# Macaron block on one core: feed-forward features and power sums written by column tiles, statistics a turn earlier

## The chip, the cores and the metric

The program runs on one core of a Trainium2 chip. Its engines work side by side, each through its own instructions in order: TensorE (PE in the profile; its weight loads are PEld), VectorE (DVE), ScalarE (ACT), GpSimd (POOL) and SyncE (SP), which here issues nearly all transfers between memory and the chip. TensorE writes only to PSUM; the others move its results on. The metric is the device time of one launch in microseconds. Three runs of the kernel before took 3954.24 us in the median (3950.4 to 3954.5).

## The reference

Four sequences of 512 tokens with 512 features pass a half-weighted feed-forward network, an attention layer of the gated delta kind, and the same feed-forward network again:

```python
x = x + 0.5 * ffn(layernorm(x), gate_cp, up_cp, down_cp)
x = x + attn(layernorm(x), W_qkvz, W_ba, conv_w, dt_bias, A_log, norm_w, W_out)
x = x + 0.5 * ffn(layernorm(x), gate_cp, up_cp, down_cp)

def ffn(h, gate_cp, up_cp, down_cp):        # layernorm: (x - mean) / sqrt(var + 1e-5)
    gate_w = spline(gate_cp)                # 2048 x 512
    up_w = spline(up_cp)                    # 2048 x 512
    down_w = spline(down_cp)                # 512 x 2048
    return (silu(h @ gate_w.T) * (h @ up_w.T)) @ down_w.T
```

Each weight matrix is a cubic spline through some 8,100 control points, about 129 weights to a segment. So 128 neighbouring weights of a row lie on one or two cubic pieces. The kernel uses that: a product with such weights needs only few combinations of the inputs. The attention is not touched by the change and takes the middle of the run.

## The kernel before

`ffn(src, dst, build)` runs twice, with `attention()` between. The first time it also builds the spline weights (`build`), the second time it loads them. In both, `B` is 4 sequences. `NC` and `NT` are 4 (chunks of 128 features, tiles of 128 tokens), `NB` is 16 (blocks of 128 hidden rows), `NG_F` is 8, `NODES` and `BLK` are 32, `P` is 128 and `S` is 512. One sequence goes through these steps:

- **Features** (`features`, lines 344 to 380). `norm(t)` normalises a tile of 128 tokens on VectorE (L355); its first call computes the statistics of the whole sequence (`statistics`, L331 to L342: BN statistics on VectorE, L336 and L337, then the power -1/2 on GpSimd, L341). `turn(t)` transposes the tile on TensorE (L362) and ScalarE copies it (L363). `interpolate(hf, c)` multiplies a 128 x 128 slice of the table `lag` with chunk `c` (L367). Its 128 output rows are 32 for each of four feature groups, but a later matmul wants, for one group, the 32 rows of all four chunks in one tile `ft[g]`. So ScalarE copies the result to a staging tile `fs` (L371, four buffers), and four transfers put its quarters into four `ft` tiles (L373). That is 8 matmuls, 8 copies and 32 transfers.
- **Hidden** (`hidden`). For each of 16 blocks a gate and an up matmul (L435, 128 x 128 x 512), SiLU on ScalarE (L442), their product on VectorE (L444), and a store of the block to `hid` in memory (L445). `gu` PSUM has two buffers, `ffn_it` has four.
- **Gather** (`gather`). Sixteen indirect transfers on GpSimd (L454) read the rows of `hid` back in another order into the tiles `nat`. The first waits until all of `hid` is stored.
- **Project** (`project`). 32 units: four `sums(k)`, each four matmuls of 32 columns (L474) with the table `pw` (powers of the position), one per `nat` tile, into the four quarters of a PSUM tile; ScalarE copies it (L478) to `fs`, and four transfers (L481) put 16 rows of each quarter into a tile `fm`. Then 16 `blocks(v)` (L491, four matmuls of 32 rows each), four `rest(g)` (L494) and eight `total(k, g)` (L497), which add up in four PSUM banks `y`. `back(g)` transposes the result (L508) and VectorE adds it to the residual `ffn_xr` in 44 steps (L536). The output is then stored (L514).

**Order.** A small calendar delays followers: `later(d, f)` runs `f` after `d` further `tick()`s. The first sequence's features and hidden blocks, and the second's features (`whole`), are issued ahead of the loop, in an order that a planner finds. From there `manual_schedule` keeps the written order on TensorE, VectorE, ScalarE and GpSimd; SyncE's order is still the planner's. In turn `b` of the loop the 16 gathers of sequence `b` come first on GpSimd. Then the 32 gate and up matmuls of hidden(b+1) are issued one by one, as slots. Woven between: `norm` for sequence b+2 at slots 0 to 3; from slot 2, up to slot 12 (`lead`), the back-transposes of sequence b-1 with the turns and interpolations of b+2; from slot 12 the units of project(b). Sequence b+2 is loaded at the start of the same turn. In turn 2 there is no sequence 4 to prepare, and the loop then issues hidden(3) first and the units of project(2) behind it, with the last 16 gathers dropped in between; turn 3 is project(3) alone.

The loop that sets this order, at the end of `ffn`, begins:

```python
nat, steps = gather(0)
for b in range(B):
    for f in steps:
        f()
    main, norms, turns, inter = [], [], [], []
    if b + 1 < B:
        main = hidden(b + 1, ft)
    if b + 2 < B:
        ft, norms, turns, inter = features(load(b + 2, "ffn_x", io))
    units, back = project(b, nat)
```

## Time and profile before

| | us |
|---|---|
| median of 3 runs | 3954.24 |
| the profiled execution | 3989.9 |
| its span, first to last instruction | 3988.1 |
| TensorE matmul busy (90% of the span) | 3608.3 |
| VectorE, ScalarE, GpSimd busy | 2628.2, 1472.2, 857.1 |
| first feed-forward stage, from to | 0 to 460 |
| second feed-forward stage, from to | 3587 to 3988 |

An engine row gives busy time in tenths of each of 40 equal slices (99.7 us each); `PEclk` is the clock that TensorE was granted, in tenths. A row of stretches has the stretch, its length, then busy time and instruction count of PE, PEld, DVE, ACT and POOL, the granted clock, the share of the transfer engines and GB/s. A timeline row has start, duration, engine, line, operation, output<-inputs and count; in brackets stands how long the engine was idle before it and what released it. A chain row has start, duration, engine, name and line. One matmul in the code is two instructions in the profile ("x2"), and four small ones are "x8". SPq and POOLq mark the issuing of transfers.

### The profile page before, as it was taken

The page shows a single profiled execution, that of the slowest core. Times are in us where ns is not written, and L with a number is a line of the kernel's source. Part 1 is how long each engine was busy: PE and PEld are TensorE (multiplying, and loading weights), DVE is VectorE, ACT ScalarE, POOL GpSimd, SP SyncE. Part 2 cuts the span into 40 slices and gives each one's busy share as a digit, 9 for nine tenths or more (in the row PEclk, how much of TensorE's full clock was granted, in tenths as well). Part 3 has the DMA queues.
Part 4 walks back from the last instruction along what each step waited for, and adds up shares of the span by engine and source line. Part 5 has one row for each costly group of instructions (what it writes and reads, how often), then busy time and mean ns, then how long its engine had stood idle before and what let it go on. Part 6 is the DMA issues. An engine that isn't in the chain of part 4 may idle for free. (4 is left out here: it accounts for less than half of the span.)

```text
span 3988.1 us, 62538 instructions
## 1 busy us (share of the span) xinstructions
PE 3608.3 (90%) x24184; PEld 2005.3 (50%) x24184; DVE 2628.2 (66%) x5925; ACT 1472.2 (37%) x3448; POOL 857.1 (21%) x662
## 2 busy tenths in 40 slices
PE   5878668999999999999999999999999999976788
PEld 2333325555555555555555555555555555542333
DVE  5222267887787888777878887787888877632221
ACT  2321113444444444444444444444444444422221
POOL 2113011222222222222222222222222222111111
PEclk7989778999999999999999999999999999978898
DMA  5535211221112222221222221122121121115353
GB/s 175 179 120 181 91 44 51 64 67 58 57 57 73 59 83 59 65 59 57 62 70 80 62 67 58 56 62 70 57 85 56 53 67 54 48 72 189 112 170 94
DMA packets 319192, 323.25 MB, mean 81 GB/s; under 512 B 102736, under 2 KB 237168, under 8 KB 318320
## 3 DMA queue, kind: packets, MB, share of 16 engines
q1 hardware_dynamic: 308656, 285.69, 23.3%
q0 software_dynamic: 10240, 33.56, 2.9%
q8 instruction: 191, 3.13, 0.3%
q14 instruction: 105, 0.86, 0.1%
HBM read 247.60 MB, written 50.59 MB: 75 GB/s over the span
## 5 line engine op out<-in xcount | busy, mean ns | idle before, releaser
L981 DVE SCALAR_TENSOR_TENSOR acc<-pj,cw,acc 128x511 f32<-128x511 f32 (+2 forms) x768 | 573.6, 747 | 151.6 <-ACT acc L979 133.4
L971 PE MATMUL pj<-xnT,w_v 128*128 128x512 f32 x1024 | 521.1, 602 | 0.0
L1286 PE MATMUL pz<-w_z,xnT 128*128 128x512 f32 x1024 | 514.6, 614 | 0.0
L1434 PE MATMUL py<-w_o,gT 128*128 128x512 f32 x1024 | 513.7, 615 | 0.4
L444 DVE TENSOR_TENSOR ffn_it<-pu,ffn_sg 128x512 f32<-128x512 f32 x128 | 88.5, 691 | 332.1 <-PE pu L435 194.5
L971 PE MATMUL pj<-xnT,w_k 128*128 128x512 f32 x512 | 265.3, 626 | 20.2 <-DMA w_k<-in_L_attn_W_qkvz 20.2
L971 PE MATMUL pj<-xnT,w_q 128*128 128x512 f32 x512 | 255.3, 602 | 0.0
L989 ACT ACTIVATE th<-acc 128x512 f32<-128x512 f32 x256 | 163.0, 637 | 235.4 <-DVE acc L981 226.3
L1342 ACT ACTIVATE tq<-pks,rqe 128x128 f32<-128x128 f32 x384 | 120.3, 364 | 339.9 <-DVE rq L1183 204.9
L1412 ACT ACTIVATE oo<-oo,orr 128x128 f32<-128x128 f32 x512 | 162.6, 389 | 206.5 <-POOL oo L1407 206.5
L979 ACT ACTIVATE acc<-pj,cw 128x512 f32<-128x512 f32 x256 | 175.3, 685 | 170.2 <-PE pj L971 169.4
L454 POOL DMA_INDIRECT nat<-hid,idx x128 | 122.0, 953 | 490.4 <-PE y_pt L508 160.6
L1434 PEld LDWEIGHTS py<-w_o,gT 128*128 128x128 f32 x1024 | 171.0, 191 | 106.2 <-issue 95.2
L1286 PEld LDWEIGHTS pz<-w_z,xnT 128*128 128x128 f32 x1024 | 169.8, 191 | 99.5 <-issue 88.5
L1012 POOL TENSOR_TENSOR rsq<-msq,phalf 128x4 f32<-128x4 f32 x64 | 64.8, 1013 | 684.8 <-DVE msq L1010 684.8
L1012 POOL TENSOR_TENSOR rsk<-msk,phalf 128x4 f32<-128x4 f32 x64 | 70.0, 1094 | 653.3 <-DVE msk L1010 651.7
L971 PEld LDWEIGHTS pj<-xnT,w_v 128*128 128x128 f32 x1024 | 170.7, 191 | 70.7 <-issue 64.1
L1168 POOL TENSOR_TENSOR ks<-kn,ws 128x1024 f32<-128x1024 f32 x64 | 122.5, 1915 | 379.2 <-DVE ws L1161 346.7
L993 DVE SCALAR_TENSOR_TENSOR vT<-th,acc 128x512 f32<-128x512 f32 x128 | 181.7, 1420 | 23.1 <-ACT th L989 23.1
L1093 DVE TENSOR_TENSOR inv<-inv,inv_tmp 128x30 f32<-128x30 f32 (+14 forms) x480 | 168.8, 352 | 16.5
L1400 DVE TENSOR_REDUCE om<-osq 128x4 f32<-128x512 f32 x128 | 87.1, 681 | 138.5 <-ACT osq L1399 138.5
L1350 PEld LDWEIGHTS pzz<-rr,tt 128*128 128x128 f32 x768 | 114.9, 193 | 113.3 <-issue 54.5
(204 smaller groups left out, 6923.6 us busy)
## 6 DMA issues: line engine op xcount, KB each, us to landing
hid<-ffn_it SPq DMA_DIRECT2D x128, 256.0 KB
w_v<-in_L_attn_W_qkvz SPq DMA_DIRECT2D x64, 512.0 KB
w_z<-in_L_attn_W_qkvz SPq DMA_DIRECT2D x64, 512.0 KB
w_o<-in_L_attn_W_out SPq DMA_DIRECT2D x32, 1024.0 KB
ab<-decay_c SPq DMA_DIRECT2D x64, 512.0 KB
ft<-fs SPq DMA_DIRECT2D x256, 64.0 KB
w_k<-in_L_attn_W_qkvz SPq DMA_DIRECT2D x64, 256.0 KB
w_q<-in_L_attn_W_qkvz SPq DMA_DIRECT2D x64, 256.0 KB
```

The source lines that it names most:

```text
L454: nc.gpsimd.indirect_dma_start(out=nt, out_offset=None, in_=to[:, :], in_offset=bass.IndirectOffsetOnAxis(ap=idx[:, v : v + 1], axis=0),)
L971: nc.tensor.matmul(pj, w()[:, c, col : col + DK], xnT[:, c, :], start=c == 0, stop=c == NC - 1)
L979: nc.scalar.activation(acc, pj, AF.Copy, scale=cw[:, ch, 3:4])
L981: nc.vector.scalar_tensor_tensor(acc[:, d:], pj[:, : S - d], cw[:, ch, 3 - d : 4 - d], acc[:, d:], ALU.mult, ALU.add)
L989: nc.scalar.activation(th, box["acc"], AF.Tanh)
L993: nc.vector.scalar_tensor_tensor(dest(), box["th"], 1.0, box["acc"], ALU.add, ALU.mult)
L1012: nc.gpsimd.tensor_tensor(rs, ms, phalf[:, :NT], ALU.pow)
L1093: nc.vector.tensor_tensor(ee[:, j + 1 :, :j], ee[:, j + 1 :, :j], tj, ALU.add)
L1168: nc.gpsimd.tensor_tensor(ks, bc(kn, 2, 2), bc(ws, 3, P), ALU.mult)
L1286: nc.tensor.matmul(pz, xnT[:, c, t * P : (t + 1) * P], pair["wz"][:, c].rearrange("p j k -> p (j k)"), start=c == 0, stop=c == NC - 1,)
L1412: nc.scalar.activation(s["oo"][:, t, r], s["oo"][:, t, r], AF.Copy, scale=s["orr"][:, u : u + 1])
L1434: nc.tensor.matmul(box["py"], pair["gT"][r][:, t, :], pair["wo"][:, r, :], start=r == 0, stop=r == 3)
```

## The change

- `interpolate` is now per feature group `g`: four matmuls of 32 columns each, one per chunk, write the four quarters of one PSUM tile, which ScalarE copies straight to `ft[g]`. The 32 transfers and `fs` go.
- `sums`: two calls share a PSUM tile. `pw` becomes two tables of 32 columns; the second has the powers in columns 16 to 31 and zeros elsewhere. Call r = 0 starts each quarter and r = 1 adds to it, and one copy writes the whole tile `fm`. The 16 transfers go. The gathered tiles that one call reads are 8m + 2j + r for j = 0 to 3, where before they were four neighbours.
- `statistics` is its own step `stats`. In the loop, sequence b+3 is loaded at slot 16 of turn `b` and its statistics are issued at slot 28, so they stand ahead of the next gathers on GpSimd.
- The loop body becomes `turn_of(b)`. The 16 gathers of the next sequence are issued at the end of a turn. In turn 2 the units of project(2) are woven into hidden(3) too, except the last 16, which follow the gathers.
- In the building stage, the second sequence's features are woven into hidden(0) from its ninth slot. In the other stage hidden(0) is a turn -1 in the hand-written order, with the same features.
- SyncE belongs to the hand-written order as well.

```diff
@@ -347,9 +347,10 @@
                 ft = [fp.tile([P, S], F32, name="ft") for _ in range(NG_F)]
                 xn, stat = {}, {}
 
+                def stats():
+                    stat["mv"], stat["rstd"] = statistics(xt)
+
                 def norm(t):
-                    if t == 0:
-                        stat["mv"], stat["rstd"] = statistics(xt)
                     mv, rstd = stat["mv"], stat["rstd"]
                     xn[t] = wk.tile([P, H], F32, name="ln_xn", bufs=3)
                     nc.vector.tensor_scalar(
@@ -362,26 +363,22 @@
                         nc.tensor.transpose(pt[:, c, :], xn[t][:, c * P : (c + 1) * P], ident)
                     later(1, lambda: nc.scalar.copy(xnT[:, :, t * P : (t + 1) * P], pt))
 
-                def interpolate(hf, c):
+                def interpolate(g):
                     pf = ps.tile([P, S], F32, name="pf", tag="tp")
-                    nc.tensor.matmul(pf, lag[:, c, hf * P : (hf + 1) * P], xnT[:, c, :], start=True, stop=True)
-
-                    def spread():
-                        fs = wk.tile([P, S], F32, name="fs", tag="fs", bufs=4)
-                        nc.scalar.copy(fs, pf)
-                        for q in range(4):
-                            nc.sync.dma_start(
-                                ft[4 * hf + q][NODES * c : NODES * (c + 1)], fs[NODES * q : NODES * (q + 1)]
-                            )
-
-                    later(1, spread)
+                    for c in range(NC):
+                        nc.tensor.matmul(
+                            pf[NODES * c : NODES * (c + 1)], lag[:, c, NODES * g : NODES * (g + 1)], xnT[:, c, :],
+                            start=True, stop=True,
+                        )
+                    later(1, lambda: nc.scalar.copy(ft[g], pf))
 
                 turns = [lambda t=t: turn(t) for t in range(NT)]
-                inter = [lambda hf=hf, c=c: interpolate(hf, c) for hf in range(2) for c in range(NC)]
-                return ft, [lambda t=t: norm(t) for t in range(NT)], turns, inter
+                inter = [lambda g=g: interpolate(g) for g in range(NG_F)]
+                return ft, stats, [lambda t=t: norm(t) for t in range(NT)], turns, inter
 
             def whole(xt):
-                ft, norms, turns, inter = features(xt)
+                ft, stats, norms, turns, inter = features(xt)
+                stats()
                 for n_, t_ in zip(norms, turns):
                     n_()
                     t_()
@@ -410,9 +407,11 @@
             wr = wdp.tile([P, NB, P], F32, name="wr")
             we = wdp.tile([P, H], F32, name="we")
             cm = wdp.tile([P, 2, H], F32, name="cm")
-            pw = wdp.tile([P, BLK], F32, name="pw")
+            pw = wdp.tile([P, 2, BLK], F32, name="pw")
             idx = wdp.tile([P, NB], mybir.dt.int32, name="idx")
-            nc.sync.dma_start(pw, grid[:, G_POW:G_IDX])
+            nc.vector.memset(pw, 0.0)
+            for e in range(2):
+                nc.sync.dma_start(pw[:, e, 16 * e : 16 * e + 16], grid[:, G_POW : G_POW + 16])
             nc.sync.dma_start(idx, grid[:, G_IDX:].bitcast(mybir.dt.int32))
             if not build:
                 nc.sync.dma_start(wr.rearrange("p c h -> p (c h)"), wr_d)
@@ -469,18 +468,15 @@
                     if k == 0:
                         box["xr"] = load(b, "ffn_xr", ip)
                         box["fm"] = [np_.tile([P, S], F32, name="fm", tag="fm", bufs=2) for _ in range(2)]
-                    pf = ps.tile([P, S], F32, name="pm", tag="tp")
+                    m, r = divmod(k, 2)
+                    if r == 0:
+                        box["pm"] = ps.tile([P, S], F32, name="pm", tag="tp")
+                    pm = box["pm"]
                     for j in range(4):
-                        nc.tensor.matmul(pf[BLK * j : BLK * (j + 1)], pw, nat[4 * k + j], start=True, stop=True)
-
-                    def spread():
-                        fs = wk.tile([P, S], F32, name="fs", tag="fs", bufs=4)
-                        nc.scalar.copy(fs, pf)
-                        for j in range(4):
-                            at = 16 * (4 * (k % 2) + j)
-                            nc.sync.dma_start(box["fm"][k // 2][at : at + 16], fs[BLK * j : BLK * j + 16])
-
-                    later(1, spread)
+                        at = slice(BLK * j, BLK * (j + 1))
+                        nc.tensor.matmul(pm[at], pw[:, r], nat[8 * m + 2 * j + r], start=r == 0, stop=r == 1)
+                    if r:
+                        later(1, lambda: nc.scalar.copy(box["fm"][m], pm))
 
                 def blocks(v):
 
@@ -543,61 +539,92 @@
                 units += [lambda k=k, g=g: total(k, g) for k in range(2) for g in range(4)]
                 return units, [lambda g=g: back(g) for g in range(4)]
 
-            for f in hidden(0, ft):
-                f()
-                tick()
-            drain()
-            built.close()
+            plan = {"nxt": None, "tail": [], "ft": ft}
+
+            def turn_of(b):
+
+
+                main = hidden(b + 1, plan["ft"]) if b + 1 < B else []
+                norms, turns, inter = [], [], []
+                if plan["nxt"]:
+                    plan["ft"], _, norms, turns, inter = plan["nxt"]
+                    plan["nxt"] = None
+                units, back = [], []
+                if b >= 0:
+                    units, back = project(b, plan["nat"])
+                plan["nat"], steps = gather(b + 1)
+                tail, early = plan["tail"], []
+                for i in range(4):
+                    early += [*tail[i : i + 1], *turns[i : i + 1]]
+                early += inter
+                lead = 6 * 2 if b >= 0 else len(main)
+                for i, f in enumerate(main):
+                    if b + 3 < B:
+                        if i == 16:
+                            xt = load(b + 3, "ffn_x", io)
+                        if i == 28:
+                            plan["nxt"] = features(xt)
+                            plan["nxt"][1]()
+                    for n_ in norms[i : i + 1]:
+                        n_()
+                    f()
+                    tick()
+                    n = -(-len(early) // max(1, lead - i)) if i < lead else 0
+                    if i >= 2 or not turns:
+                        for f in early[:n]:
+                            f()
+                            tick()
+                        early = early[n:]
+                    if i >= lead:
+                        keep = 16 if b + 2 == B else 0
+                        n = -(-(len(units) - keep) // (len(main) - i))
+                        for f in units[:n]:
+                            f()
+                            tick()
+                        units = units[n:]
+                drain()
+
+                for f in steps if b + 1 < B else ():
+                    f()
+                for f in early + units:
+                    f()
+                    tick()
+                plan["tail"] = back
+
+            by_hand = lambda: tc.manual_schedule(
+                engines={e.engine for e in (nc.tensor, nc.vector, nc.scalar, nc.gpsimd, nc.sync)}
+            )
+            if B > 1:
+                xt = load(1, "ffn_x", io)
+                plan["nxt"] = features(xt)
+                plan["nxt"][1]()
+            if build:
+                first = hidden(0, plan["ft"])
+                ft, _, norms, turns, inter = plan["nxt"] or (None, None, [], [], [])
+                more = [f for nt in zip(norms, turns) for f in nt] + inter
+                xt2 = load(2, "ffn_x", io) if B > 2 else None
+                for i, f in enumerate(first):
+                    f()
+                    tick()
+                    for f in more[:1] if i >= 8 else ():
+                        f()
+                        tick()
+                        more = more[1:]
+                drain()
+                plan["ft"], plan["nxt"] = ft, None
+                if B > 2:
+                    plan["nxt"] = features(xt2)
+                    plan["nxt"][1]()
+                built.close()
             np_ = st.enter_context(tc.tile_pool(name="ffn_nat", bufs=NB + 4))
-            ft = whole(load(1, "ffn_x", io)) if B > 1 else None
-            tail = []
-            with tc.manual_schedule(engines={e.engine for e in (nc.tensor, nc.vector, nc.scalar, nc.gpsimd)}):
...
+            with by_hand():
+                if build:
+                    plan["nat"], steps = gather(0)
                     for f in steps:
                         f()
...
+                for b in range(0 if build else -1, B):
+                    turn_of(b)
+                for f in plan["tail"]:
                     f()
                     tick()
                 drain()
```

## The prediction

> **What bounds the kernel.** I began with the rows of tenths: attention (about 460 to 3587 us of the span) keeps TensorE near nine tenths and is not touched; the two feed-forward stages have holes. Then one row per stage of the second one, cut where a turn's first gate matmul starts. "Turn 0" is hidden(1) with project(0) woven in, "turn 1" hidden(2) with project(1).
>
> ```profile
> PE   5878668999999999999999999999999999976788
> PEclk7989778999999999999999999999999999978898
> ```
>
> ```profile
> core 0: us, PE busy (x) PEld busy (x) DVE busy (x) ACT busy (x) POOL busy (x), PEclk, DMA share, GB/s
> ...
> 3661.25:3755.08 93.83, 71.76 (x280) 28.23 (x279) 12.60 (x20) 20.29 (x36) 16.41 (x17) 0.87 0.45 138
> 3755.08:3856.33 101.25, 75.29 (x295) 30.32 (x294) 22.57 (x74) 20.39 (x36) 16.25 (x17) 0.87 0.43 130
> 3856.33:3977.23 120.90, 109.55 (x477) 43.59 (x475) 25.26 (x112) 19.52 (x33) 30.31 (x32) 0.90 0.43 141
> ```
>
> TensorE is the busiest engine by far, and a turn holds 22 to 26 us in which it stands. The timeline of turn 1 says why:
>
> ```profile
> 3757.75 0.60 PE L508 MATMUL y_pt<-ident,yg 128*128 128x128 f32 x4
> 3758.26 1.02 POOL L454 DMA_INDIRECT nat<-hid,idx  x1 [75.54 <-DMA hid<-ffn_it]
> ...
> 3777.10 0.95 POOL L454 DMA_INDIRECT nat<-hid,idx  x1 [0.30 <-issue]
> 3778.07 1.04 POOL L341 TENSOR_TENSOR ln_rstd<-ln_var,phalf 128x4 f32<-128x4 f32 x1
> 3779.15 1.00 DVE L355 TENSOR_SCALAR ln_xn<-ffn_x,ln_mv,ln_rstd 128x512 f32<-128x512 f32 x2 [20.37 <-issue]
> 3779.84 1.09 PE L362 MATMUL ln_pt<-ident,ln_xn 128*128 128x128 f32 x4 [21.49 <-DVE ln_xn L355]
> ```
>
> The power for 1/std (1.04 us on GpSimd) sits behind 16 gathers, 1.25 us apart. Normalising on VectorE waits for it, the transposes wait for that, and TensorE, in written order, waits 21.5 us with ready matmuls behind. A second hole comes later in the turn:
>
> ```profile
> 3798.39 7.47 SPq L373 DMA_DIRECT2D ft<-fs  x12
> ...
> 3802.29 0.59 ACT L371 COPY fs<-pf 128x512 f32<-128x512 f32 x1 [2.38 <-DMA ft<-fs]
> ...
> 3803.43 1.12 PE L435 MATMUL pg<-ft,wc 128*128 128x512 f32 x2 [2.33 <-ACT ffn_sg L442]
> ```
>
> Each feature copy is followed by four transfers at 0.6 us of SyncE; the fifth copy needs a staging buffer back, and the SiLU and then the gate matmul queue behind the copy.
>
> **Cost of a column-tiled group.** The chain shows four 128x32 matmuls of 512 columns (two passes each, x8) beside a full one (x2):
>
> ```profile
> 3716.19 1.07 PE y L491 x8
> 3717.26 1.00 PE pm L474 x8
> 3718.26 1.05 PE pg L435 x2
> ```
>
> Here a group takes 1.00, elsewhere 1.12; a full matmul is 0.86, 1.05 right after tiled work. Against the change speaks the Trainium skill, "TensorEngine Tiling (Array Packing)", Key Properties: changing the tiling mode drains the engine, and the new features do so 16 times per sequence. It states no figure. But the row already stands between two switches: at worst 1.12 for the group and 1.05 - 0.86 on the full matmul behind it, 1.31. So a group costs 1.00 to 1.31, most rows lie near the low end, and I take 1.06: 8 x (1.06 - 0.86) = +1.6 us per sequence, 13 in all. Were the rule a further price, say one 0.43 us pass at each switch, it would be 7 us per sequence, 55 in all, and the forecast 3825 would read 3880; nothing in the row asks for that.
>
> **Part 1, statistics one turn sooner.** Moved are 4 x (0.67 + 0.18) + 0.17 = 3.6 us of VectorE, 1.04 us of GpSimd and the 1 MB load of x on SyncE. The load goes from the gathers' time to slot 16 of the turn before, in a stretch at 66 to 74 GB/s; 12 slots of over 1 us cover it. The power now stands ahead of the gathers, whose own start still waits for the last hidden store (3758.26, about 3.2 us after the turn's first matmul). Removed are the waits: 19.6 + 1.8 (restart at half pace) in turn 0, 21.6 + about 2.5 in turn 1. The power moved ahead of 16 gathers delays none of them, since they start later than it ends. Queued behind the moved statistics is ffn_it of that slot, hence the next up matmul: 3.6 us less about 2 of slack, 1.5 us, three times (4.5; bounds 0 to 11).
>
> **Part 2, no chip transfers.** 384 SyncE issues of about 0.6 us and 21 MB go; one clearing of the power table and one more small load per stage come, at a start where larger loads cover them. What returns to TensorE is the copy wait: from 3702.45 to 3715.06 there are 7.7 us of work in 12.6 (4.9 us) in turn 0, and likewise 7.3 us in turn 1. PSUM copies: eight for features stay eight; sums need two for four, 1.2 us of idle ScalarE. The sums still run 16 small matmuls; their accumulation needs gathers 8, 10, 12, 14 for the third sum (before 8 to 11). Gather 14 is issued about 3.2 + 14 x 1.25 + 1 = 21.7 us into a turn and lands by 24 to 26; TensorE reaches that sum at 12 x 0.86 + 1.75 + 1.75 + 8.5 + 0.86 + 2 + 0.86 + 1.07 = 27. Hidden barely; I charge 1 us in each of four turns (0 to 5).
>
> So turn 0 becomes 93.8 - 19.6 - 1.8 - 4.9 + 1.6 = 69.1, turn 1 101.25 - 21.6 - 2.5 - 7.3 + 1.6 = 71.5. Sums of rows agree: hidden 27.5, turns 1.75, features 8.5, sums 4, blocks 15.5 and switches 1.6, rest and totals 10.3, which is 69.2. In the first stage the same turns last 80.6 (gathers started under other work) and 101.1.
>
> **Part 3, the last two turns.** Before, from 3856.33 to 3975.5: 119.1 us, as hidden(3) runs with nothing between (1.97 us a pair against 1.72, and 8 us of waits) and each projection runs alone (37.5 us each). After: hidden(3) 27.5 + back-transposes 1.75 + 16 units 17 + pace 1.4 = 47.6. Then 16 kept units (14.3 us), under which the last gathers start 3.2 us in. TensorE is at the third sum of project(3) after 14.3 + 1.75 + 2 + 1.07 + 3.2 (the y banks wait for VectorE, as before) = 22.3; gather 14 lands near 25.5, after which 27 us of projection remain: 53. Together 100.6, a gain of 18.5; in the first stage 123.3 - 100.6 = 22.7. Without the kept units as cover, the gather wait would be 14 us longer.
>
> **Part 4, starts.** Second stage, first features to turn 0: 52.75. After: eight groups 8.5, hidden 27.5, turns 1.75, features 8.5, VectorE pace 2.2, about 0.6 at the seams: 49, gain 3.7. In the first stage hidden(0) with the weight build is 71.2 us and whole(1) follows to 88.7; woven in, 10.3 us of TensorE work goes partly into gaps of 0.9 us per two blocks: 79 (76 to 84), gain 9.7. At its very start, four late feature matmuls (44.57 to 48.2) held the coefficient transposes 5.5 us; VectorE and GpSimd follow (0 to 6), I take 3. SyncE by hand inside the stages: behind the output store, which waits for the 44 VectorE additions, stand the hidden stores; four buffers of 3 us and more cover it. At the seams with attention the weight loads may no longer pass the last store: -4 to +4 us, taken as 0.
>
> **What comes new.** Hidden stores now share the transfer engines with the gathers. "DMA: Bandwidth & Descriptors", Issuing engines are not separate DMA queues, says that transfers from any issuing engine share 16 engines and interleave, and this speaks against the change. The trace has one such stretch, hidden(3) over gathers:
>
> ```profile
> 3867.79 11.86 SPq L445 DMA_DIRECT2D hid<-ffn_it  x4
> ...
> 3878.61 0.69 DVE L444 TENSOR_TENSOR ffn_it<-pu,ffn_sg 128x512 f32<-128x512 f32 x1 [6.92 <-remote]
> ...
> 3879.36 2.07 PE L435 MATMUL pu<-ft,wc 128*128 128x512 f32 x2 [3.25 <-issue]
> ```
>
> It lost 8.0 us idle and about 2 cold. By the rule as full competition, each of six turns (three a stage) pays 10, and the forecast would be 3870. By pace, the new turns store every 3.7 us against 2 and load no residual meanwhile: I take 2.5 x 6 = 15 (0 to 60).
>
> **Sum**, against the profiled span of 3988.1 (execution 3989.9): 3 + 9.7 + 11.5 + 29.6 + 22.7 + 3.7 + 24.7 + 29.7 + 18.5 = 153.4; less 15 + 4.5 + 4 = 23.5: 129.9. The median shown, 3954.24, is 0.991 of that execution, so 128.7 off it: **3825**.
>
> **Rivals.** (a) *Stores and gathers collide fully*: 60 for 15, late gathers 16 for 4: net 73, 3882. For it, transfers at 0.91 share there; against it, half the store rate and 21 MB fewer bytes. (b) *All is covered*: none of the 23.5 appears, 3802. (c) *Slower*: the feature tiles do not overlap. Four in a row cost 3.44 a group, 2.38 more x 64 = 152, net +22: 3976. It decides from 1.06 + 130/64 = 3.1 us a group. The sums' tiles of the same shape overlap, though each has its own moving tile where the features' four read slices of one. (d) *The change doesn't do what it says*: the 21 us wait only moves from the transposes to the sums, in three turns 63 us: net 67, 3888. For it, the sums wait for the same gathers; against it, they come 23 to 27 us into a turn.
>
> **Chances.** Main case 0.55 (3802 to 3850), (a) 0.20 (3850 to 3900), (b) 0.17 (3780 to 3802), (c) 0.04, (d) 0.04. A measurement of this kernel tells some 0.2% from no change; a quarter of (c), tiles that overlap partly, ends within it: faster 0.96, within 0.01, slower 0.03. The range 3783 to 3876 leaves out about 2 in 10: half of (a), (c), (d) and the low edge of (b).
>
> **What would show it.** Right: ln_rstd before the first gather, ln_pt with no wait on ln_xn, turns of 70 to 75 us in the second stage, feature groups near 1.06 us, no staging rows. Wrong: feature matmuls of 3 us a group, hidden stores late for ffn_it by 8 us a turn, or sums waiting on gathers. The forecast falls most easily on the 15 us for transfers and on the last gathers.

## The result, and the profile after

The changed kernel took **3886.7 us** in the median (3884.7 to 3887.2); the kernel before, beside it, took 3954.3 (3950.4 to 3954.5). The ratio is 0.983, with an interval of 0.9813 to 0.9847. It is faster by 68 us where the forecast said 129, and it ends above the range.

The pictures of the two executions differ by more than that: the spans are 3988.1 and 3885.4, a difference of 102.7. The rest of this document is about these two gaps. One has to know for it that the runs fall into two kinds, by the chip they met: on some the kernel before takes 3948 to 3958 us in the median, on others, called the slower chips below, 3976 to 3987. Each time is therefore compared with the kernel before on the same chip; where stretches of two chips are put side by side, the text says so.

First the tenths of TensorE and of its clock, after the change:

```profile
PE   5998569999999999999999999999999999987998
PEclk7999679999999999999999999999999999997999
```

Attention fills the middle as before; both ends have filled up. The stretches of the second feed-forward stage, cut at the same instructions as before (turn 0, turn 1, turns 2 and 3; the columns are those explained above):

```profile
core 0: us, PE busy (x) PEld busy (x) DVE busy (x) ACT busy (x) POOL busy (x), PEclk, DMA share, GB/s
3613.14:3685.79 72.65, 71.76 (x326) 24.69 (x327) 16.45 (x30) 18.55 (x33) 16.97 (x18) 1.00 0.45 149
3685.79:3757.49 71.70, 71.70 (x343) 26.48 (x342) 19.19 (x65) 19.33 (x34) 15.20 (x16) 1.00 0.42 147
3757.49:3872.60 115.11, 103.53 (x461) 36.58 (x460) 23.95 (x105) 16.60 (x28) 30.26 (x32) 0.97 0.44 149
```

Turn 1 has no idle time left. The timeline of its start shows why; this answers the rows in which the transposes waited 21.5 us:

```profile
3682.57 1.04 POOL L341 TENSOR_TENSOR ln_rstd<-ln_var,phalf 128x4 f32<-128x4 f32 x1 [45.79 <-DVE ln_var L339]
3688.88 1.02 POOL L453 DMA_INDIRECT nat<-hid,idx  x1 [5.27 <-DMA hid<-ffn_it]
...
3688.90 0.60 PE L363 MATMUL ln_pt<-ident,ln_xn 128*128 128x128 f32 x4
...
3695.49 1.06 PE L369 MATMUL pf<-ffn_xnT,lag 128*32 128x512 f32 x8
```

The power is done 5.3 us before the first gather, the transposes carry no wait, and a feature group costs the 1.06 us of the forecast. What is new is in the waits of TensorE (engine and line, what it waited for, us in total, times, longest), first stage and then second:

```profile
PE pm L477 <- DMA nat<-hid,idx: 14.8, 8, 5.8
...
PE pm L477 <- DMA nat<-hid,idx: 11.1, 7, 3.7
```

The power sums wait for gathered tiles, 15 times. The kernel before has no such row in the run before_c (below), whose profile gives the landings of its gathers; the profile of the forecast gives none, so its silence alone would not say much. Stage by stage, in us of the two profiled executions:

| stretch | before | after | forecast |
|---|---|---|---|
| FFN1: hidden(0), features(1) | 88.7 | 76.0 | 79 |
| FFN1: turn 0 | 80.6 | 79.9 | 69.1 |
| FFN1: turn 1 | 101.1 | 71.7 | 71.5 |
| FFN1: turns 2 and 3 | 123.3 | 116.6 | 100.6 |
| FFN2: first features to turn 0 | 52.8 | 52.7 | 49 |
| FFN2: turn 0 | 93.8 | 72.7 | 69.1 |
| FFN2: turn 1 | 101.3 | 71.7 | 71.5 |
| FFN2: turns 2 and 3 | 119.0 | 115.1 | 100.6 |

The holes that the change aimed at are gone at the price forecast. Turns 2 and 3 are 16.0 and 14.5 us too long, turn 0 of the first stage 10.8.

### The profile page after: what moved, and what is told of

Same layout as the page of the kernel before. It is cut to its first block, busy times and chain, and to the rows that moved or that the text cites. A ratio compares the mean times of both kernels' runs of the same rounds, so it can differ in the third digit from the quotient of the medians.

```text
span 3885.4 us, 62488 instructions
## 1 busy us (share of the span) xinstructions
PE 3594.6 (93%) x24568; PEld 1975.0 (51%) x24568; DVE 2631.4 (68%) x5927; ACT 1463.3 (38%) x3432; POOL 855.7 (22%) x662
```

## Experiments

**Parts alone, on one chip (kernel before there: 3987.3).** Theory: the stage table, with the excess put down to sums that wait for gathers. Rivals: transfers that collide (rival a), and a start value that does not hold. First the kernel before once more.

> The kernel before, unchanged. Its first profiled execution took 3989.9 us, its other runs 3950 to 3955. If that one execution was slow by chance, this one shows about 3955, and a comparison by stages says where 35 us went. If it is bound to the profile (for instance because this kernel issues many more transfers), it is again near 3990 while the runs beside it stay near 3954. My forecast assumed a slowdown spread evenly over the whole run.

3987.4 us, span 3985.5: on this chip the first profile is the ordinary case, and the 3954 of the median is not. Stage by stage the two profiles agree as well (turns 2 and 3 take 123.7 and 117.3 us here, 123.3 and 119.0 there). On which chip the first was taken is not on record; that it was one of the slower kind is a conclusion from these times.

The column tiles alone, in the order of before:

```diff
-                    nc.tensor.matmul(pf, lag[:, c, hf * P : (hf + 1) * P], xnT[:, c, :], start=True, stop=True)
...
+                    for c in range(NC):
+                        nc.tensor.matmul(
+                            pf[NODES * c : NODES * (c + 1)], lag[:, c, NODES * g : NODES * (g + 1)], xnT[:, c, :],
```

> The kernel before with column-tiled features and sums and no chip transfers; loop, statistics and SyncE's order as before. By my steps: the staging waits go (about 19 us in four turns and some 15 at the stage starts), the tiles cost 13, the wait of the power behind the gathers stays: 20 us off, 3934. If the sums then wait for gather 14 in place of the staging waits, nothing is left: 3950 to 3955.

3954.8 us, ratio 0.992 (0.9906 to 0.9939): 32.5 us gained, more than the 20 of its first theory; 14.7 of them lie between hidden(0) and turn 0 of the first stage. The statistics alone, one turn sooner, staging and transfers kept:

```diff
+                            if i == 16:
+                                xt = load(b + 3, "ffn_x", io)
+                            if i == 28:
+                                nxt = features(xt)
+                                nxt[1]()
```

> The kernel before with load and statistics one turn sooner and nothing else. By my steps the 21 us wait goes in three turns and 5 us in the fourth: up to 65 us off, 3890. If the wait only moves to the sums, which need the same gathers, a third of it is left: 3930 or more.

3956.2 us, ratio 0.992 (0.9907 to 0.994): 31 us, less than half of the 66.9 us for which the transposes wait in the first profile (4.7, 21.5, 19.3 and 21.5), and between what the two theories gave. A stand, that is a stretch of idle time, like that of the run after_again, below, takes 10.5 and 11.1 us of the two second turns. Then the changed kernel with each pair of sums moved behind eight blocks, so that the sums that read gathers 8 to 15 come last:

```diff
-                units = [lambda: sums(0), lambda: sums(1), lambda: blocks(0), lambda: sums(2)]
-                units += [lambda v=v: blocks(v) for v in range(1, 4)] + [lambda: sums(3)]
+                units = [lambda v=v: blocks(v) for v in range(NB // 2)] + [lambda: sums(0), lambda: sums(1)]
+                units += [lambda v=v: blocks(v) for v in range(NB // 2, NB)] + [lambda: sums(2), lambda: sums(3)]
```

> The changed kernel with the sums moved behind the blocks of the same gathered tiles (two after the eighth block, two after the sixteenth), and the residual's load with them. If late gathers are what the last two turns and the first stage's turn 0 lost (in its profile 8 us in that turn, about 5 in each turn 2 and 8 to 10 in each turn 3), 25 to 35 us go: 3852 to 3862. If the last turns are long by tile switches and VectorE's pace, at most 8 go: 3879 or more.

3929.7 us, ratio 0.986 (0.984 to 0.9873): by its ratio no better than the change itself, and far from the 3852 to 3862 of its first theory. Turn 1 takes 85.3 and 85.2 us in the two stages instead of 71.7, with a stand of 11.1 and 9.6 us in front of the first feature group. This profile gives no landing of a gather, so it cannot tell whether the sums still waited. The changed kernel was then run on such a chip too.

**Suspected transfers, on a chip where the kernel before takes 3982.5.**

> The changed kernel unchanged, beside its variants on one chip. Theory 1 (what a chip adds lies on both kernels alike): ratio to the kernel before again 0.981 to 0.985, so about 3887 us where the kernel before takes 3954, and about 3920 us where it takes 3987. Theory 2 (the changed kernel meets nothing of what makes the kernel before slower there): 3887 us on either, a ratio of 0.975 where the kernel before takes 3987.

3930.5 us, ratio 0.988 (0.9847 to 0.9907), nearer to theory 1; the changed kernel loses on such a chip as well, 44 us against 28. Its stretches, and the place in turn 1 of the first stage that the last one starts from:

```profile
3623.65:3706.56 82.91, 73.22 (x326) 25.01 (x327) 16.45 (x30) 18.43 (x33) 16.96 (x18) 0.94 0.40 130
3706.56:3792.06 85.50, 74.35 (x344) 26.86 (x343) 19.28 (x65) 19.22 (x34) 15.18 (x16) 0.94 0.37 123
3792.06:3911.02 118.96, 106.19 (x461) 38.00 (x460) 24.45 (x105) 16.48 (x28) 30.26 (x32) 0.93 0.43 144
```

```profile
219.61 0.60 ACT L441 ACTIVATE ffn_sg<-pg 128x512 f32<-128x512 f32 x1
231.88 0.58 ACT L364 COPY ffn_xnT<-ln_pt 128x512 f32<-128x512 f32 x1 [11.67 <-remote]
...
219.95 0.60 PE L363 MATMUL ln_pt<-ident,ln_xn 128*128 128x128 f32 x4
220.39 1.02 PE L434 MATMUL pg<-ft,wc 128*128 128x512 f32 x2
232.52 3.54 PE L369 MATMUL pf<-ffn_xnT,lag 128*32 128x512 f32 x16 [11.11 <-issue]
```

Turn 1 takes 85.5 us instead of 71.7. ScalarE stands 11.7 us in front of a copy whose only input, the transposes at 219.95, seems long done by the rows, and TensorE waits for the copy. The release is given as "remote": the profile names no instruction for it (more on this under what stays open). All of it lies inside the 20 us in which GpSimd issues gathers, and turn 1 of the second stage has the same stand (10.2 us) at the same copy. Three suspects on the same chip. The hidden stores at an eighth of their bytes:

```diff
-                    nc.sync.dma_start(to[k * P : (k + 1) * P, :], it)
+                    n = S if b == 0 else S // 8
+                    nc.sync.dma_start(to[k * P : (k + 1) * P, :n], it[:, :n])
+                    if build and b == 0:
+                        nc.sync.dma_start(hid[1][k * P : (k + 1) * P, :], it)
```

> The changed kernel with the hidden stores of every turn that has gathers beside it cut to an eighth of their bytes (hidden(1) to hidden(3) of both FFNs; the gathers then read old rows, so the output is not the reference's; hidden(0) of FFN1 stores each tile a second time, to fill the other buffer, with no gather beside it). Theory 1 (rival a of the prediction, gathers and stores compete for the transfer engines): the waits of the sums and the coming and going of ffn_it shrink, FFN1 T0 from 79.9 to 72 to 75 us, hidden(3) from 58.7 to 52 to 55 us in each FFN, the whole 15 to 30 us less than the changed kernel on the same chip. Theory 2 (the gathers are paced by their own 4.2 MB and their own issue): less than 6 us.

The residual load moved from the first sum to the first `rest`:

```diff
                 def rest(g):
+                    if g == 0:
+                        box["xr"] = load(b, "ffn_xr", ip)
...
                     if k == 0:
-                        box["xr"] = load(b, "ffn_xr", ip)
```

> The changed kernel with the 1 MB residual load of each turn issued behind the last block product instead of with the first sum. Theory 1 (the load stands in the way of the last gathers): gathers 14 and 15 land some 3 to 4.5 us sooner (1 MB at the 230 to 300 GB/s of that stretch), worth 8 to 20 us over the turns in which a sum waits. Theory 2 (it only fills gaps): within 3 us of the changed kernel. Against both: a residual that comes too late for the additions would cost up to 5 us a turn.

And turn 2 in its old order:

```diff
-                    if i >= lead:
-                        keep = 16 if b + 2 == B else 0
+                    if i >= lead and b + 2 < B:
+                        keep = 0
...
+                    for g_ in steps[: 4 if i == 0 else i >= 8] if b + 2 == B else ():
+                        g_()
+                        steps = steps[1:]
```

> The changed kernel with its turn 2 as before (all units of project(2) behind hidden(3), the last gathers 4 and then 1 a unit). Theory 1 (the new order of the end is worth what the prediction charged it with, 17 to 19 us a FFN less the 15 us that went missing there): the whole 4 to 12 us more than the changed kernel. Theory 2 (the new order gains nothing, what T2+T3 gained came from the tiles alone): within 3 us, or less time.

3933.0, 3932.5 and 3927.0 us (ratios 0.9875, 0.9876, 0.9861, each by 0.003 either way): none differs from 3930.5, as the second theory of each had said. TensorE's stand behind the same copy remains in all three (9.7 to 11.0 us in the first stage). So it does not come of the bytes of the stores (there were as many stores as before), and rival (a) as a collision of stores and gathers finds no support: taking away 7/8 of the bytes that were to collide gained nothing. And on this kind of chip the new order of turn 2 gains nothing over the old.

**The burst of gathers, on a chip where the kernel before takes 3947.6.**

> The changed kernel unchanged, as the measure for the three beside it. If this chip makes the kernel before take about 3985 us, the second turns with 86 us each and the 11 us in which ScalarE stands still in front of the last ffn_xnT copy come again (3930 us); if it makes it take 3954, they are gone and the second turns take 72 us (3887 us).

3882.4 us, ratio 0.984 (0.9818 to 0.9856); turns 0 and 1 of the second stage take 72.3 and 71.7, without a stand. This chip is of the kind of the result. Beside it, gathers of an eighth of the bytes in turns 1 and 2:

```diff
+                    thin = b in (1, 2)
+                    n = S // 8 if thin else S
+                    nt = n0[v] if thin else np_.tile([P, S], F32, name="nat")
...
-                        out=nt, out_offset=None, in_=to[:, :],
+                        out=nt[:, :n], out_offset=None, in_=to[:, :].rearrange("r (a c) -> (r a) c", c=n),
```

> The changed kernel with the gathers for blocks 1 and 2 (those of turns 1 and 2) fetching an eighth of their columns, from another view of the same buffer, so that the output is not the reference's; as many gathers as before, each issued by GpSimd as before; the gathers for blocks 0 and 3 are whole. On a chip where the second turn of the changed kernel takes 86 us: theory 1 (the standstill of ScalarE comes of the bytes that the gathers move): turn 1 takes 72 to 75 us in both FFNs and the whole 25 to 32 us less than the changed kernel. Theory 2 (it comes of GpSimd issuing them, whatever they move): turn 1 still takes 84 to 88 us, the whole within 6 us. Where the second turn takes 72 us anyway: 2 to 8 us from the gather waits of turn 2, nothing else.

3877.4 us: 5 us less, as said for such a chip; the sums in hidden(3) of the second stage wait 0.9 us instead of 3.1. Then the sums behind the blocks and the last eight gathers issued one by one, and the whole burst held back:

```diff
+                    if plan["pend"] and k >= plan["from"]:
+                        dm = wk.tile([P, 4], F32, name="dm")
+                        nc.gpsimd.tensor_tensor(dm, it[:, :4], it[:, :4], ALU.mult)
+                        for _ in range(plan["n"]):
+                            plan["pend"].pop(0)()
```

> The changed kernel with the power sums behind eight blocks each (as in the run sums_late) and the last eight gathers of turns 0 to 2 issued one by one, each behind an ffn_it tile of the next hidden (a GpSimd product of 4 columns that reads the tile holds the queue), instead of all sixteen in a row. Theory 1 (it is the burst that hurts): where the changed kernel's second turn takes 86 us it falls to 74 to 80 us, and the whole is 15 to 35 us below the changed kernel. Theory 2 (each gather hurts by itself, or the burst is harmless): within 6 us of the changed kernel, or worse by the late landing of the last ones.

> The changed kernel with the power sums behind eight blocks each and all sixteen gathers of turns 0 to 2 held back until the fourth ffn_it tile of the next hidden, then issued in a row: the burst moved some 13 us later. Theory 1 (the standstill goes with the burst): no stall at the last ffn_xnT copy of turn 1, but one of some 10 us elsewhere, 5 to 17 us behind the first gather, and a turn of about 86 us again where the changed kernel's is 86. Theory 2 (it belongs to that place of the code): the ScalarE stall stays in front of the last ffn_xnT copy. The wait for the gathers themselves may add up to 10 us a turn.

3853.5 (ratio 0.976, 0.974 to 0.9777) and 3861.3 us (0.978, 0.9756 to 0.9795). There was no stand to thin out here, so theory 1 of both was not put to its test, and yet they gained 29 and 21 us against after_c. What the two share is the place of the sums.

**The place of the sums, and the stages of the kernel before, on a chip where that takes 3958.2.**

> The changed kernel with each pair of power sums behind eight blocks, gathers in one burst: what the run spread shares with it. On a chip where the changed kernel takes about 3885 us: if the sums' wait for gathers 7 to 15 is all that is lost, this alone gives 3853 to 3860 us as spread did; if the thinning of the burst gives it, 3875 to 3885. Where the changed kernel takes 3930: 3925 to 3930 as before.

> The run spread again beside its half. On a chip where the kernel before takes about 3950 us: a ratio of 0.974 to 0.978 again. Where it takes about 3985 us: if the burst of gathers is what stops ScalarE there, the second turns fall from 86 to 72 to 78 us and the whole is 3855 to 3880 us, a ratio of 0.968 to 0.974; if not, 3895 to 3930 us.

> The run thin_gathers again (gathers of turns 1 and 2 with an eighth of their columns, old rows; the output is not the reference's). Where the kernel before takes about 3985 us: turn 1 at 72 to 75 us if the bytes of the gathers stop ScalarE, at 84 to 88 us if their issue does. Where it takes about 3950 us: 3874 to 3880 us as before.

> The kernel before, once more with its profile, to see its stages where it takes about 3950 us. Theory 1 (the profiled execution that the forecast stood on held stalls that the shorter runs do not have, in the turns with gathers): span about 3950 us, attention the same 3070 us within 6, FFN2 T0 and T1 each 5 to 15 us below the 93.8 and 101.3 of the first profile, and the like in FFN1. Theory 2 (all of the program is a little faster there): the 35 us lie in attention in proportion. Where it takes about 3985 us again: the stages of the first profile.

The sums alone give 3850.4 us, ratio 0.974 (0.9721 to 0.9754), all of what spread gives (3854.3, ratio 0.975), and slightly more than the first expectation of sums_late had said for such a chip; thin_gathers came out at 3878.0. The kernel before took 3959.3: theory 1 had the size and the wrong place. Its second stage, and below it that of sums_late_c, in the same three stretches:

```profile
3645.72:3740.40 94.68, 72.11 (x280) 28.47 (x278) 12.60 (x20) 20.27 (x36) 16.43 (x17) 0.87 0.45 137
3740.40:3841.66 101.26, 75.27 (x295) 30.43 (x294) 22.55 (x74) 20.38 (x36) 16.26 (x17) 0.87 0.44 130
3841.66:3947.61 105.95, 98.62 (x462) 39.42 (x461) 24.00 (x105) 18.91 (x32) 30.32 (x32) 0.95 0.49 161
```

```profile
3589.29:3659.67 70.38, 70.38 (x327) 24.76 (x328) 16.46 (x30) 18.55 (x33) 16.96 (x18) 1.00 0.47 153
3659.67:3731.02 71.35, 71.35 (x344) 26.68 (x342) 19.21 (x65) 19.33 (x34) 15.21 (x16) 1.00 0.44 148
3731.02:3835.03 104.01, 99.74 (x462) 40.90 (x461) 23.94 (x105) 16.60 (x28) 30.27 (x32) 0.97 0.49 165
```

Two things stand here. For the kernel before, turns 0 and 1 are as in the first profile (93.8 and 101.3), but turns 2 and 3 take 105.95 instead of 119.0; in the first stage they take 107.2 instead of 123.3. And with the sums moved, turn 0 is 70.4 in both stages, with no idle time. Some of the 13 us lie in plain sight when the same blocks of project(2) are put beside each other, first from the profile of the forecast, then from before_c:

```profile
3908.43 6.10 PE L491 MATMUL y<-nat,wr 32*128 32x512 f32 x46
3915.25 0.58 PE L491 MATMUL y<-nat,wr 32*128 32x512 f32 x1 [0.72 <-issue]
3915.98 1.25 PE L491 MATMUL y<-nat,wr 32*128 32x512 f32 x3
3918.06 1.70 PE L491 MATMUL y<-nat,wr 32*128 32x512 f32 x3 [0.82 <-issue]
3920.15 7.57 PE L491 MATMUL y<-nat,wr 32*128 32x512 f32 x41 [0.40 <-issue]
```

```profile
3889.51 10.57 PE L491 MATMUL y<-nat,wr 32*128 32x512 f32 x94
```

The same blocks take 19.3 us in the one and 10.6 in the other; hidden(3) ahead of them holds most of the rest. The first is full of short waits whose release reads "issue". They add up to 1.9 us; the rest is longer busy time, at a lower granted clock, as the stretches of these blocks show (first profile, then before_c):

```profile
3908.43:3927.72 19.29, 17.20 (x99) 6.94 (x95) 0.00 (x0) 0.59 (x1) 12.86 (x15) 0.82 0.67 191
3889.51:3900.08 10.57, 10.57 (x99) 4.88 (x95) 0.00 (x0) 0.58 (x1) 7.83 (x10) 1.00 0.74 217
```

Waits and lower clock come together here; no run takes them apart.

**The old end with and without the early sums.** Two more runs were to tell the new order of the end from the sums in it; they met a chip on which the kernel before takes 3976.

> The changed kernel with its turn 2 as before (all units of project(2) behind hidden(3), the last gathers 4 and then 1 a unit), again. On a chip where the kernel before takes about 3955 us and its stretch from hidden(3) to the end of FFN2 116 us against 125 of the changed kernel: if the new order of the end is what loses there, that stretch falls to 110 to 116 us, the one of FFN1 from 118 to 103 to 108, the whole to 3855 to 3868 us, a ratio of 0.974 to 0.980. If the sums' wait loses it in either order: within 5 us of the changed kernel, a ratio of 0.982 to 0.985. Where the kernel before takes about 3985 us: a ratio of 0.986 as before.

> Both at once: each pair of power sums behind eight blocks, and turn 2 as before. On a chip where the kernel before takes about 3955 us: if the two cure the same wait, 3845 to 3855 us, a ratio of 0.973 to 0.975, as sums_late_c alone; if they add up, 3830 to 3842 us, a ratio of 0.969 to 0.972. Where it takes about 3985 us: 3920 to 3930 us.

3929.1 and 3918.6 us, ratios 0.987 (0.9849 to 0.9899) and 0.984 (0.9815 to 0.9867). That does not answer the question for the faster kind, for which it was asked. On this chip, with the old end, the place of the sums is worth 10.5 us; the runs of the two (3928.0 to 3931.9 and 3911.8 to 3921.5) do not overlap.

## Why the prediction was wrong

**Column tiles: right.** Feature groups take 1.06 us. A price per change of mode beyond the row (3880), which the Trainium skill's page "TensorEngine Tiling (Array Packing)", Key Properties, had made one think of, and tiles that do not overlap (rival c) are both out.

**Parts 1 and 2, turns 0 and 1: right in the second stage** (72.7 and 71.7 against 69.1 and 71.5), and for turn 1 in the first. With the sums moved they are 70.4 and 71.35. The wait for the power did not move to other work (rival d): turn 1 has no wait at all. That the measured 3886.7 lies beside the 3888 of rival (d) and the 3882 of rival (a) is chance; of the latter, the late gathers came true, the colliding stores did not.

**The step that failed is part 3.** It set 119.1 and 123.3 before against 100.6 after. Both sides were off. (1) *The start value.* On a chip of the result's kind the kernel before spends 105.95 and 107.2 there: 13.0 and 16.1 us less, together 29.1. The spans of the two profiles differ by 27.7 (3988.1 and 3960.4), so this is all of it. The prediction had seen that its execution was 36 us above the median and answered with a factor of 0.991 on the gain, worth 1.2 us. The excess was not spread over the program; it lay in two stretches that the change was credited with shortening, and came off the gain in full. (2) *The end value.* After the change turns 2 and 3 take 115.1 and 116.6, 30.5 us more than twice 100.6. The forecast put hidden(3) with its 16 units at 47.6 us and what follows at 53. The second stage of after_c in these two parts, and below it that of sums_late_c (two chips of the faster kind):

```profile
3752.24:3810.41 58.17, 53.72 (x213) 16.55 (x211) 16.85 (x60) 11.32 (x19) 15.16 (x16) 1.00 0.49 179
3810.41:3867.13 56.72, 51.62 (x253) 20.77 (x254) 7.17 (x45) 5.28 (x9) 15.17 (x16) 0.94 0.38 119
```

```profile
3731.02:3783.11 52.09, 50.72 (x213) 16.43 (x211) 16.83 (x60) 10.74 (x18) 15.12 (x16) 1.00 0.57 199
3783.11:3835.03 51.92, 49.03 (x254) 24.48 (x254) 7.11 (x45) 5.86 (x10) 15.14 (x16) 0.93 0.41 130
```

Moving the sums behind the blocks brings the 114.9 down to 104.0, and in the first stage 118.7 to 109.6: 20 of these us are the sums' place. Put against 105.95 and 107.2, the new end as shipped *loses* 8.9 and 11.5 us where 18.5 and 22.7 of gain were forecast.

**Behind the end value stand the landings of the gathers.** The profile at hand showed none. Part 2 had the issue of gather 14 start 20.7 us into a turn and end at 21.7, and let it land "by 24 to 26", 3.3 to 5.3 us after that start; no row was behind the figure. In the profile after, the landings of turn 0 of the first stage are given with their least, middle and most, counted from the start of the issue:

```profile
L453 POOL DMA_INDIRECT nat<-hid,idx x16: 942/946/1197, 139.0 to 158.0; - x16
...
DMA to landing us min/median/max: 4.0/4.5/10.6
```

In the other turns it is 3.3 to 7.9, and 5.0 in the median of the kernel: the middle was guessed well, the late end was left out. In this turn the first gather also starts 5.2 us into the turn instead of 3.2, and gather 14 takes the 10.6 us. The third sum stands 5.8 us for it and starts at 167.44, 33.6 into the turn, and the turn is 10.8 us over. Of that, after_c and sums_late_c (75.6 and 70.4) show 5.2 as the sums'. In the two turns 1 gather 14 lands at 26.0 and 26.9, just ahead of the sum at 27.7.

In turn 2 the forecast has no wait for a gather at all; that term was put at nothing without a reason. There no features of another sequence stand ahead of the sums, so they come at 15.4, 19.7 and 23.9 us into the turn, and wait (after_c, second stage, turn from 3752.24):

```profile
3769.89 1.04 PE L477 MATMUL pm<-nat,pw 128*32 128x512 f32 x2 [1.24 <-DMA nat<-hid,idx]
...
3778.20 1.04 PE L477 MATMUL pm<-nat,pw 128*32 128x512 f32 x2 [1.04 <-DMA nat<-hid,idx]
3780.04 1.04 PE L477 MATMUL pm<-nat,pw 128*32 128x512 f32 x2 [0.79 <-DMA nat<-hid,idx]
```

The prediction charged the sums 4 us in turns 0 and 1 and allowed 3.2 in each turn 3, some 10 in all. Their place cost 5.2 and 1.9 in the two turns 0, 0.35 in each turn 1, and 9.1 and 10.9 in turns 2 and 3: nearly 28, and 20 of them in the last two turns.

**What was charged too high.** 15 us for colliding stores: turn 1 has no such loss on a chip of the result's kind (71.7 against 71.5 without any charge), and thin stores gained nothing. **Smaller:** hidden(0) with woven features 76.0 for 79; first features to turn 0 of FFN2 gained 0.1 for 3.7. With the sums moved, hidden(3) still takes 52.1 us for 47.6: 1.4 of that is idle time, and 14 to 16 times a full matmul behind a tiled one at 1.05 for 0.86 us, some 3 us a stage, was in the shown row and left out of the 47.6. In the first stage what follows hidden(3) takes 57.6 for 53.

The account, in us of profiled spans: forecast gain 129.6 (the terms of the sum add up to 153.1, not 153.4); less 29.1 for the start value, 30.5 for the end value, 10.8 and 3.6 for the turns 0, 3.7 for the second start; plus the 23.5 of charges, since the stages are compared with the forecast without them, and 3.0 for hidden(0): 78.4. Another 4.8 went at the first start (1.4), in the turns 1 (0.4) and at the seam before the second stage (3.0, taken as 0): 73.6, which is the 102.7 between the two spans less the 29.1. The span after is 75.0 below that of before_c, after_c's 80.5. In the medians of the result it is 67.6. The execution of before_c (3962.1) is 8 us above the 3954.3 there; where these 8 us lie is not known.

**What stays open.** The slower chips: what holds TensorE and ScalarE for 11 us, and TensorE between small matmuls. The trace of after_again, which also has the times of the semaphore updates by which engines release each other, says more than its rows. The results `pu`, `y_pt` and `ln_pt` of TensorE that end at 219.68, 220.12 and 220.55 by the rows are signalled at 221.93, 224.82 and 231.86, each later than the one before. VectorE goes on at 222.01 and 224.84, ScalarE at 231.88, each right behind its signal. In after_c the same signals stand within 0.05 us of the ends. So it is TensorE that ends late, or signals late, and ScalarE waits as it should; since the ends of matmuls are modelled in these profiles, they do not tell which.

The slower traces also lack events. Of the semaphore updates by transfers the profile of the forecast has 20,294 and before_c 22,658. In turns 2 and 3, where the times differ, it is 689 and 680 against 1413 and 1299; in attention, where they agree, 10,896 against 10,909. (The turn 0 of the second stage lacks some too, 1174 against 1568, without being longer.) In after_again turn 1 of the second stage has 282 of them where after_c has 544, and the stretch from hidden(0) to turn 0, which takes as long on both, has 240 and 240. With events missing no landing can be told: the 11 profiles of slower chips have no landing time of a gather, the 9 others have them:

```profile
nat<-hid,idx POOLq DMA_INDIRECT x128
nat<-hid,idx POOLq DMA_INDIRECT x128, 4.5
```

(before, then before_c.) Whether the recording of the events itself holds the engines there, or one cause makes both, no run tests. No chip was met a second time, so it is not shown either that it is the chip and not the hour. Thin stores, a late residual load and the old end did not cure the stands; thin gathers and the spread burst met only chips without them. Open too is whether the old end would be better still on the faster kind.

**A better version.** The changed kernel with each pair of sums behind eight blocks takes 3850.4 us, a ratio to the kernel before of 0.974 (0.9721 to 0.9754) where the change as shipped has 0.983 and 0.984; the intervals do not meet. On the slower chips the two are alike (0.986 and 0.988).

## What to carry to other kernels

When a profiled execution is slower than the median, find the stretch that holds the excess before forming differences from it; if the change touches that stretch, the excess comes off the gain whole, not by a factor. Here the profile held a sign: its gathers have no landing time. A transfer counts from issue to landing, and a landing that no row shows needs a wide bound: here it was 3.3 to 10.6 us where 3.3 to 5.3 was assumed, and the last one decides. When an order is moved to a turn with less work ahead of it, the waits of that turn have to be worked out anew. Consumers of data that arrive one tile at a time go in the order of arrival, those that need the last tiles at the end.

## What was not expected of the hardware

The two kinds of chips differ by place, not throughout. From the first transposes of attention to the first ffn_it tile behind it the kernel before takes 3148.3 us in the first profile and 3149.5 in before_c, and its turns 0 and 1 agree within 1.2 us too, gathers and all. Its turns 2 and 3 take 13.0 and 16.1 us more in the first profile. In the changed kernel a turn takes up to 14 us more (85.5 for 71.7), with a signal of TensorE 11.3 us behind the modelled end; on the other kind turn 1 has no idle time. The stretches that are longer also lack events in the trace. Fewer bytes did little: seven eighths of the gathered bytes of four turns were worth 5 us on the faster kind.
